# A Nystrom attention and expert block on one core: the routing loss from products over tokens, the inverse in pairs of rounds

## The chip, the cores and the metric

The kernel runs on one core of one Trainium2 chip. A core has TensorE (matmuls, PE), VectorE (DVE), ScalarE (ACT), GpSimd (POOL) and SyncE (SP, which issues DMAs). Matmuls write to PSUM, eight banks of 2 KB per partition; everything else lies in SBUF, 128 partitions. All data are fp32, and an fp32 matmul stands in the trace as two passes, each with its own weight load (PEld). The metric is device microseconds of one execution.

## The reference

The input is x of 16 batches, 1024 tokens, 256 features. Two residual layers follow each other:

```python
x = x + layernorm(attn(layernorm(x)))
x = x + layernorm(ffn(layernorm(x)))
```

The attention is Nystrom's, with 16 heads of 16 features and 64 landmarks (means over 16 neighbouring tokens). Three softmax kernels are formed, k1 (tokens by landmarks), k2 (landmarks by landmarks) and k3 (landmarks by tokens), and k2 is inverted by six rounds:

```python
V = K.T / max(colsum(K))
for _ in range(6):
    KV = K @ V
    V = 0.25 * V @ (13*I - KV @ (15*I - KV @ (7*I - KV)))
out = (k1 @ V) @ (k3 @ v) @ w_proj
```

The second layer chooses one of eight experts per batch, by how well a small autoencoder of each expert reconstructs the normalised tokens, and adds that expert's adapter to a common base layer:

```python
h = relu(x @ Wd1[e] + bd1[e])            # 256 -> 64, for all 8 experts
recon = h @ Wd2[e] + bd2[e]              # 64 -> 256
idx = argmin_e mean((recon - x)**2)      # per batch
out = x @ W_base + b_base + relu(x @ Wa_down[idx] + ba_down[idx]) @ Wa_up[idx] + ba_up[idx]
```

## The kernel before

The work of a batch is written as four stages, each a Python generator. `stage_a` turns the normalised x, makes queries, keys and values, and sums k3 against the values. `stage_p` forms k2 and inverts it. `stage_c` forms k1, multiplies, projects, normalises and adds. `stage_d1` normalises again and computes the eight losses, the choice and the gathers of the expert's weights; `stage_d2` computes base and adapter, normalises, adds and stores.

Each stage yields, ahead of a piece of work, a tuple from `go(...)`: its name, the pieces it follows, and its costs on the engines (`mm(us, mode, n)` for TensorE, `ew(engine, us, ...)` for others). At the end of the kernel a planner (`Model`, `first`, `planned`, lines 1089 to 1210) merges the stages of different batches into one order: it tries each piece that may come next, runs its model forward for `AHEAD` us under a few rules, and takes the piece that loses least TensorE time. The order is then emitted as it stands (`tc.manual_schedule`), so each engine's queue has this order. There are five streams (line 1053): stage a of all batches, stage p of the even batches, stage p of the odd batches, stage c, and stages d1 and d2. PSUM tiles come from one pool of four buffers of two banks (`ps2`), taken in turn.

TensorE's array is used in several tile shapes, which the trace gives as rows*columns: 128*128, 64*64 (four products side by side), 32*128 and 128*32 (four), 128*64 (two).

In `stage_p` a head's matrix is 64 by 64, and 16 heads lie in one [128, 8, 64] tile. `product` (line 552) multiplies all 16 heads, 32 passes of 64 columns in 64*64 tiles; it can place its result in one or the other half of the partitions, which the next product's operands need. A round (line 630) has the steps kv (two products, K V placed in two ways, then two subtractions from 7/3 of the identity on VectorE, yx and yy), sq (one product), t3 (one product) and v (two products, V and its transpose, each scaled by ScalarE). Every step waits for the one ahead of it. Tiles of stage p carry the batch's parity in their tags, so that two batches have their own.

In `stage_d1` the hidden layer is made per pair of experts: `hidden` (line 895) writes ph, 128 hidden units by 1024 tokens, and ScalarE applies bias and relu (ht, line 907). Then for each pair, half of the features and half of the tokens, a group pr (line 932) of eight passes reconstructs two experts' 128 features of 512 tokens, VectorE subtracts xt (df, line 940) and ScalarE squares with a bias and sums along the row (line 943, with a second instruction that reads the accumulator). A batch has four ph groups and 16 pr groups. `pe` (line 961) adds the sums per expert, a matmul with ones (pl, line 966) adds over partitions, and the choice and the gathers on GpSimd follow.

Ahead of the first batch the weights are loaded on ScalarE's DMA queue and the first x on SyncE's; VectorE centres w_proj and w_base (lines 154 to 156), and two small transposes bring the biases into columns (line 192).

## Time and profile before

| | |
|---|---|
| median of three runs | 2420.9 us (2420.38 to 2425.7) |
| profiled execution, its own time | 2422.45 us |
| its span | 2420.7 us |
| PE / PEld busy | 2220.6 us (92%) / 1458.7 us (60%) |
| DVE / ACT / POOL busy | 1475.8 (61%) / 1241.5 (51%) / 272.2 us (11%) |
| mean granted clock of TensorE | 0.978 |
| loss: pr (L932), df (L940), squares (L943) busy | 251.0 PE, 301.7 DVE, 363.3 ACT us |
| hidden layer: ph (L899), ht (L907) | 236.3 PE, 70.8 ACT us |
| inverse: the products of the six rounds (L563, without pkt) | 380.5 us PE, in 18432 passes |

Busy time of a group counts an instruction from its start to its modelled end. Matmuls overlap their successors, so groups of PE add up to more than the time they take from their start to the next group's start; the timeline shows the latter. The granted clock is the share of TensorE's full clock that the chip let through. "Idle before" a group is put down to what ended last.

### The profile page before, as it was taken

To read this page: it belongs to the slowest core of one execution; us is meant where nothing else is said; L and a number is where in the kernel's file an instruction comes from. 1 tells how busy PE (TensorE), PEld (TensorE's weight loads), DVE (VectorE), ACT (ScalarE), POOL (GpSimd) and SP (SyncE) were. 2 spreads that over 40 slices of the span, in tenths; PEclk is the share of its full clock that TensorE was granted. 3 is DMA by queue.
4 is the path that set the end of the run, shared out by engine and by line. 5 is a ranking of instruction groups with operands and counts; after the bars stand their busy time and mean duration, and the time that the engine had idled before them with its cause. 6 is when DMAs were issued, how large, how long until landed. Compare 5 with 4: busy or idle time off the path is not lost.

```text
span 2420.7 us, 94984 instructions
## 1 busy us (share of the span) xinstructions
PE 2220.6 (92%) x43954; PEld 1458.7 (60%) x43954; DVE 1475.8 (61%) x2811; ACT 1241.5 (51%) x2467; POOL 272.2 (11%) x387
## 2 busy tenths in 40 slices
PE   5998999999999999999999999899999999898865
PEld 3666656575565756657565665656666575665442
DVE  4556576575747666576566657557575666655443
ACT  1333464564546556464745545455454555465545
POOL 1000011020110201011020200202011020111021
PEclk9999999999999999999999999999999999999888
DMA  3000001010010100101010010101001000010000
GB/s 109 19 21 3 20 5 55 2 34 25 5 54 3 57 2 5 54 6 54 2 57 2 14 45 3 55 3 32 27 5 55 2 21 21 5 38 26 15 21 20
DMA packets 56628, 60.94 MB, mean 25 GB/s; under 512 B 4964, under 2 KB 55208, under 8 KB 56232
## 3 DMA queue, kind: packets, MB, share of 16 engines
q1 hardware_dynamic: 50208, 50.35, 6.5%
q8 instruction: 345, 5.65, 0.9%
q0 software_dynamic: 2560, 2.14, 0.3%
q10 hardware_dynamic: 3464, 2.37, 0.3%
q14 instruction: 51, 0.42, 0.1%
HBM read 38.08 MB, written 16.78 MB: 23 GB/s over the span
## 4 chain that ended last, share of the span: by engine, by line
PE 43%; DVE 8%; ACT 7%; issue 2%; POOL 1%; DMA 0%; POOLq 0%; DVEq 0%; ACTq 0%
PE ph L899 5%; PE pq L339 5%; PE pr L932 4%; ACT df L943 3%; PE pf L1033 3%; PE po L829 2%; PE pv L360 2%; PE pvi L563 2%; PE pf L1034 2%; PE pkv L563 2%; PE psv L781 2%; PE psct L752 2%; DVE df L940 2%; DVE mx L417 1%; PE psct L760 1%
## 5 line engine op out<-in xcount | busy, mean ns | idle before, releaser
L943 ACT ACTIVATE df<-df,bd_sb 128x512 f32<-128x512 f32 x512 | 363.3, 711 | 165.4 <-DVE df L940 165.4
L940 DVE TENSOR_TENSOR df<-pr,xt_d 128x1024 f32<-128x1024 f32 x256 | 301.7, 1216 | 107.9 <-PE pr L932 68.5
L932 PE MATMUL pr<-ht,wd_sb 64*64 64x512 f32 x2048 | 251.0, 597 | 3.6 <-ACT ht L907 1.5
L899 PE MATMUL ph<-xt_d,wd_sb 128*128 128x512 f32 x512 | 236.3, 604 | 1.4 <-DVE maxima L722 0.8
L339 PE MATMUL pq<-xt_a,wqkv_sb 128*128 128x512 f32 x512 | 228.1, 600 | 0.0
L722 DVE TENSOR_REDUCE maxima<-psc 128x16 f32<-128x1024 f32 x128 | 150.3, 1217 | 76.9 <-PE psc L714 76.9
L770 ACT ACTIVATE e<-psct 128x1024 f32<-128x1024 f32 x128 | 124.0, 1020 | 115.3 <-PE psct L760 115.2
L417 DVE TENSOR_REDUCE mx<-psm 128x2 f32<-128x1024 f32 x128 | 149.7, 1216 | 33.5 <-PE psm L408 33.5
L339 PEld LDWEIGHTS pq<-xt_a,wqkv_sb 128*128 128x128 f32 x512 | 96.0, 192 | 114.3 <-issue 110.0
L899 PEld LDWEIGHTS ph<-xt_d,wd_sb 128*128 128x128 f32 x512 | 93.1, 191 | 117.1 <-issue 94.6
L453 ACT ACTIVATE e<-psc 128x1024 f32<-128x1024 f32 x128 | 122.8, 1025 | 73.2 <-PE psc L443 71.8
L1033 PE MATMUL pf<-wbase_sb,xt_d 128*128 128x256 f32 x512 | 136.6, 390 | 0.9 <-DVE t L659 0.9
L563 PEld LDWEIGHTS pkv<-vi,k2t 64*64 64x64 f32 x6144 | 104.1, 137 | 44.1 <-issue 18.2
L283 DVE SCALAR_TENSOR_TENSOR y_d<-y_d,rstd_d_y,x 128x256 f32<-128x256 f32 x128 | 53.3, 479 | 124.2 <-POOL rstd_d_y L250 124.1
L248 POOL TENSOR_SCALAR ve_c_y<-ss_c 128x4 f32<-128x4 f32 x32 | 6.2, 195 | 1086.6 <-ACT square_c L294 1086.6
L563 PE MATMUL pkv<-vi,k2t 64*64 64x64 f32 x6144 | 115.1, 223 | 8.0 <-ACT vi L673 3.3
L932 PEld LDWEIGHTS pr<-ht,wd_sb 64*64 64x64 f32 x2048 | 64.9, 133 | 95.5 <-issue 60.6
L829 PE MATMUL po<-wproj_sb,svt 128*128 128x256 f32 x512 | 120.1, 388 | 1.0 <-ACT svt L804 0.9
L781 PE MATMUL psv<-w_bd,e 128*32 128x34 f32 x8192 | 90.3, 198 | 33.0 <-issue 23.5
L781 PEld LDWEIGHTS psv<-w_bd,e 128*32 128x32 f32 x8192 | 80.0, 109 | 61.7 <-issue 35.7
L360 PE MATMUL pv<-wqkv_sb,xt_a 128*128 128x256 f32 x512 | 116.7, 381 | 0.0
L360 PEld LDWEIGHTS pv<-wqkv_sb,xt_a 128*128 128x128 f32 x512 | 95.9, 190 | 22.5 <-issue 7.8
(174 smaller groups left out, 4042.8 us busy)
## 6 DMA issues: line engine op xcount, KB each, us to landing
xa<-in_L_attn_x_dram SPq DMA_DIRECT2D x16, 1024.0 KB
x<-in_L_attn_x_dram SPq DMA_DIRECT2D x16, 1024.0 KB
out_dram<-y_d SPq DMA_DIRECT2D x32, 512.0 KB
wqkv_sb<-in_L_attn_w_qkv_dram ACTq DMA_DIRECT2D x1, 768.0 KB
wd_sb<-in_L_ffn_Wd_dram ACTq DMA_DIRECT2D x2, 256.0 KB
wd_sb<-in_L_ffn_Wd_dram ACTq DMA_DIRECT2D x1, 512.0 KB
wdn<-in_L_ffn_Wa_down_dram,row POOLq DMA_INDIRECT x32, 2.7
wproj_sb<-in_L_attn_w_proj_dram ACTq DMA_DIRECT2D x1, 256.0 KB
```

The costliest lines, as they stand in the source:

```text
L339: nc.tensor.matmul(pq[:, n, :], lhsT=wqkv_sb[:, k, f0 : f0 + P], rhs=xt[:, k, n * 512 : (n + 1) * 512], start=(k == 0), stop=(k == NC - 1),)
L360: nc.tensor.matmul(pv[:, j, :], lhsT=xt[:, k, (t0 + j) * P : (t0 + j + 1) * P], rhs=wqkv_sb[:, k, 2 * D : 3 * D], start=(k == 0), stop=(k ...
L417: nc.vector.tensor_reduce(mx3[:, n, q : q + 2], psc[g], X, ALU.max)
L563: nc.tensor.matmul(dst[64 * h[to] : 64 * h[to] + 64, 4 * h[frm] + 2 * g0 + g1, :], lhsT=x[rows, i, :], rhs=y[rows, j, :] if y_at else y[ro ...
L722: nc.vector.tensor_reduce(mx[:, t0 : t0 + 2, 64 * g : 64 * g + 64].rearrange("x t (p j) -> x p t j", p=2)[:, :, :, 0 : 2 * NC], psc[g].rea ...
L781: nc.tensor.matmul(psv[rows32(g), j // 2, col : col + 2 * (HD + 1)], lhsT=es[p // 2][:, p % 2, j * P + 32 * g : j * P + 32 * g + 32], rhs= ...
L829: nc.tensor.matmul(po[:, j, :], lhsT=svt[n][:, c, j * P : (j + 1) * P], rhs=wproj_sb[:, c, :], start=(c == 0), stop=(c == NC - 1),)
L899: nc.tensor.matmul(ph[:, n, :], lhsT=wd1_sb[:, k, 2 * i : 2 * i + 2, :].rearrange("p e h -> p (e h)"), rhs=xt[:, k, n * 512 : (n + 1) * 51 ...
L932: nc.tensor.matmul(pr[to, r, :], lhsT=wd2_sb[half, i, k * P + 64 * f : k * P + 64 * f + 64], rhs=ht[half, cols], start=True, stop=True,)
L940: nc.vector.tensor_tensor(df, pr, middle(xt[:, k, cols], 2), ALU.subtract)
L943: nc.scalar.activation(df[:, r, :], df[:, r, :], AF.Square, bias=bd2_sb[:, e, k : k + 1], accum_out=part[:, e, k * NW + n : k * NW + n + 1],)
L1033: nc.tensor.matmul(po[:, j, :], lhsT=xt[:, k, cols], rhs=wbase_sb[:, k, :], start=(k == 0), stop=False)
```

## The change

The loss is computed from products over tokens. With g = max(h, -bd1), which is relu(h + bd1) - bd1, a constant vector c = bd1 Wd2 + bd2 per expert, and x the normalised tokens, the squared error summed over tokens is made of g'g (64 by 64 per expert) weighted by Wd2 Wd2', g'x (64 by 256) weighted by -2 Wd2, the sums of g and of x weighted by vectors, and the sum of x squared. `hidden` now puts tokens on partitions (128 tokens by 512 hidden units of all experts) and VectorE writes the maximum into one of two tiles g0, g1, which have a column of ones behind each expert's 64. `over_tokens` makes, for a window of 512 tokens and four experts, the pg group: two experts side by side in 128*64 tiles, 256 columns against x and 65 against g with its ones, summed over four token tiles in PSUM. VectorE multiplies the result by the weights `loss_w` in place, and ScalarE sums along the rows. Sums of x come from the copies of xt (now two per window, with a sum), sums of squares from the variances. `prepare_d` makes the weights once.

The inverse treats its rounds in pairs. An even round keeps X = K V and forms t3 as before, but in place of the next K V it multiplies X by t3 (step x); the odd round then needs no product with K. The second placement of y is no longer a product: ScalarE copies two halves across partitions (`across`). Stage p of all batches is one stream, and its tiles are no longer kept per parity.

The rest: the first x comes in two loads; centring and the bias transposes move into the planned order (`prepare_c`, `prepare_d`); wd2 lies in a buffer of tag e1 that is released afterwards; the planner looks 70 us ahead, and for the last 250 us of TensorE's work to the end, with four more rules there.

```diff
-AHEAD, GAP = 50.0, 1.0
+AHEAD, LAST, GAP = 70.0, 250.0, 1.0
...
-        nc.sync.dma_start(out=t, in_=x[b].rearrange("(t p) d -> p t d", p=P))
+        rows = x[b].rearrange("(t p) d -> p t d", p=P)
+        for h in range(2 if b == 0 else 1):
+            part = slice(0, NT) if b else slice(4 * h, 4 * h + 4)
+            nc.sync.dma_start(out=t[:, part, :], in_=rows[:, part, :])
...
-    wd2_sb = const.tile([P, E // 2, D], F32, name="wd2_sb")
+    wd2_sb = work.tile([P, E // 2, D], F32, tag="e1", name="wd2_sb")
...
-    for c in range(NC):
-        centre(wproj_sb[:, c, :])
-        centre(wbase_sb[:, c, :])
...
+    loss_w = const.tile([P, E // 2, LW], F32, name="loss_w")
+    loss_x = const.tile([P, NC, E], F32, name="loss_x")
+    loss_b = const.tile([P, E], F32, name="loss_b")
+    halfmask = groups("halfmask", 2)
+    minus_bd1 = const.tile([P, E, 64], F32, name="minus_bd1")
+    nc.scalar.dma_start(out=minus_bd1.rearrange("p e h -> p (e h)"), in_=bd1.rearrange("(o e) h -> o (e h)", o=1).to_broadcast([P, E * 64]))
+    nc.vector.tensor_scalar(minus_bd1, minus_bd1, -1.0, None, ALU.mult)
+    gs = [const.tile([P, 4, E, 65], F32, name=f"g{i}") for i in range(2)]
+    for t in gs:
+        nc.gpsimd.memset(t.rearrange("p j e h -> p (j e h)"), 1.0)
+    def prepare_c():
+        yield go(("c", 0, "weights"), [("a", 0, "qk", 0, 0)], ew("dve", 1.9, None))
+        for c in range(NC):
+            centre(wproj_sb[:, c, :])
...
+        w2t_ps = two_banks([P, E // 2, NC, P], "w2t_ps")
+        for i in range(E // 2):
+            for k in range(NC):
+                nc.tensor.transpose(w2t_ps[:, i, k, :], wd2_sb[:, i, k * P : (k + 1) * P], ident)
...
+        nc.scalar.mul(loss_w[:, :, 65:LW], wd2_sb, -2.0)
...
+        ww_ps = one_bank([P, E // 2, P], "ww_ps")
+        for i in range(E // 2):
+            for k in range(NC):
+                nc.tensor.matmul(ww_ps[:, i, :], lhsT=w2t[:, i, k, :], rhs=w2t[:, i, k, :], start=(k == 0), stop=(k == NC - 1))
...
+            if squares is not None:
+                mv, rstd = stats[h]
+                nc.vector.tensor_tensor(squares[:, h, :], mv[:, :, 1], rstd, ALU.mult)
+                nc.vector.scalar_tensor_tensor(squares[:, h, :], squares[:, h, :], float(D), rstd, ALU.mult, ALU.mult)
...
+            for k in range(NC):
+                nc.scalar.activation(
+                    xt[:, k, h * 512 : (h + 1) * 512],
+                    pt[:, k].rearrange("p j c -> p (j c)"),
+                    AF.Copy,
+                    accum_out=sums[:, k, h : h + 1],
+                )
...
-        x, y = "r", "s"
...
+        f, h, g = "t", "r", "s"
+        def taken_y(px, scale):
+            y = mat("yx")
+            if scale == 1.0:
+                nc.vector.tensor_tensor(y, px, middle(eyes[0], NP), ALU.subtract)
+            else:
+                nc.vector.scalar_tensor_tensor(y, px, scale, middle(eyes[0], NP), ALU.mult, ALU.subtract)
+            return y
+        def across(y):
+            other = mat("yc", "across")
+            frm, to = (t.rearrange("x (f k p) m -> x f k (p m)", f=2, k=2) for t in (y, other))
+            for r, half in halves():
+                nc.scalar.copy(to[64 - 64 * r : 128 - 64 * r, :, r, :], frm[half, :, 1 - r, :])
+            return y, other
+        ACROSS = ew("act", 0.33, -1, "aside"), ew("act", 0.33, -1, "aside")
         for i in range(N_ITER):
-            yield step(f"kv{i}", mm(2 * Q, "q64", 128), ew("dve", 0.6, 0), ew("dve", 0.6, 0, "free aside"))
...
+            if i % 2 == 0:
+                n = 2 if i == 0 else 1
+                yield step(
+                    f"kv{i}",
+                    mm(n * Q, "q64", 64 * n),
+                    ew("dve", 0.6, 0),
+                    ew("act", 0.5, 0, "aside" if i == 0 else "free aside"),
+                    *([ew("act", 0.5, 0, "free aside")] if i == 0 else []),
+                    *ACROSS,
+                )
+                px, pvt = banks_of(f"pkv{i}")
+                x_at = product(px, (k2t, kt_at), (vi, v_at), h, (g, "p2"))
+                if i == 0:
+                    vt_at = product(pvt, (vi, v_at), (eye, None), h, (g, "p2"))
+                y = taken_y(px, 1.0)
+                xh = mat("xx")
+                nc.scalar.copy(xh, px)
+                if i == 0:
+                    vt = mat("vt")
+                    nc.scalar.copy(vt, pvt)
+                y = across(y)
+            yield step(f"sq{i}", mm(Q, "q64", 64), ew("dve", 0.6, -1, "free"))
             psq = banks_of(f"psq{i}")
-            sq_at = product(psq[0], (yx, at_x), (yx, at_x), y, ("p2", "t"))
+            sq_at = product(psq[0], (y[0], x_at), (y[0], x_at), g, ("p2", f))
             sq = mat("vi", "sq")
             nc.vector.tensor_tensor(sq, psq[0], middle(eyes[1], NP), ALU.subtract)
-            if i == 0:
-                vt = mat("vt")
-                nc.scalar.copy(vt, pvt[1])
             yield step(f"t3{i}", mm(Q, "q64", 64), ew("dve", 0.6, -1, "free"))
             pb = banks_of(f"pb{i}")
-            t3_at = product(pb[0], (sq, sq_at), (yy, at_y), x, ("p2", "t"))
-            t3 = mat("yx", "t3")
+            assert x_at == (h, (f, g, "p2"))
+            t3_at = product(pb[0], (sq, sq_at), ((*y, h), (g, (f, h, "p2"))), h, ("p2", f))
+            t3 = mat("vi", "t3")
             nc.vector.tensor_tensor(t3, middle(eyes[2], NP), pb[0], ALU.subtract)
-            more = i < N_ITER - 1
...
+            if i % 2 == 0:
+                yield step(f"x{i + 1}", mm(2 * Q, "q64", 128), ew("dve", 0.65, 0), ew("act", 0.5, 0, "free aside"), *ACROSS)
+                px, pv = banks_of(f"px{i}")
+                x_at = product(px, (xh, x_at), (t3, t3_at), g, (f, "p2"))
+                vt_at = product(pv, (t3, t3_at), (vt, vt_at), g, (f, "p2"))
+                f, h, g = h, g, f
+                y = taken_y(px, 0.25)
+                vt = mat("vt")
+                nc.scalar.mul(vt, pv, 0.25)
+                y = across(y)
+            else:
+                more = i < N_ITER - 1
+                yield step(
+                    f"v{i + 1}",
+                    mm(*((2 * Q, "q64", 128) if more else (Q, "q64", 64))),
+                    ew("act", 0.5, 0),
+                    ew("act", 0.5, 0, "free aside" if more else "free"),
+                )
+                pv = banks_of(f"pvi{i}")
+                if more:
+                    v_at = product(pv[0], (vt, vt_at), (t3, t3_at), g, (f, "p2"))
+                vt_at = product(pv[1], (t3, t3_at), (vt, vt_at), f, (g, "p2"))
+                if more:
+                    vi = mat("vi")
+                    nc.scalar.mul(vi, pv[0], 0.25)
+                vt = mat("vt")
+                nc.scalar.mul(vt, pv[1], 0.25)
+                f, h, g = g, f, h
...
+        QC = 2
+        def hidden(n, q):
+            yield go(
+                ("d", b, "g", n, q), [("d", b, "xt", n)], mm(3.44, "full", 16), ew("dve", 1.13, -1, "free")
+            )
+            ph = two_banks([P, QC, E * 64], f"ph_{b}_{n}_{q}")
+            for j in range(QC):
+                t = 4 * n + QC * q + j
                 for k in range(NC):
                     nc.tensor.matmul(
-                        ph[:, n, :],
-                        lhsT=wd1_sb[:, k, 2 * i : 2 * i + 2, :].rearrange("p e h -> p (e h)"),
-                        rhs=xt[:, k, n * 512 : (n + 1) * 512],
+                        ph[:, j, :],
+                        lhsT=xt[:, k, t * P : (t + 1) * P],
+                        rhs=wd1_sb[:, k].rearrange("p e h -> p (e h)"),
                         start=(k == 0),
                         stop=(k == NC - 1),
                     )
-            ht = work.tile([P, N], F32, tag="ht", name=f"ht_{b}_{i}")
...
+            nc.vector.tensor_tensor(
+                gs[n % len(gs)][:, QC * q : QC * q + QC, :, 0:64],
+                ph.rearrange("p j (e h) -> p j e h", h=64),
+                minus_bd1.unsqueeze(1).to_broadcast([P, QC, E, 64]),
+                ALU.max,
+            )
+        def over_tokens(n, w):
+            yield go(
+                ("d", b, "fw", n, w),
+                [("d", b, "g", n, q) for q in range(4 // QC)],
+                mm(4.4, "c64", 128),
+                ew("dve", 0.8, -1),
+                ew("act", 0.9, -1, "free"),
+            )
+            g = gs[n % len(gs)]
+            pf = two_banks([P, 2, 512], f"pg_{b}_{n}_{w}")
+            for i in range(2):
+                for cols, own in ((slice(65, LW), False), (slice(0, 65), True)):
+                    for j in range(4):
                         for r, half in halves():
+                            e = 4 * w + 2 * i + r
                             nc.tensor.matmul(
-                                pr[to, r, :],
-                                lhsT=wd2_sb[half, i, k * P + 64 * f : k * P + 64 * f + 64],
-                                rhs=ht[half, cols],
-                                start=True,
-                                stop=True,
+                                pf[half, i, cols],
+                                lhsT=g[:, j, e, 0:64],
+                                rhs=g[:, j, e, :] if own else xns[n][:, j, :],
+                                start=(j == 0),
+                                stop=(j == 3),
                             )
-                    df = buf4k("df", [P, 2, 512], f"df_{b}_{i}_{k}_{n}", 3)
...
+            fw = pf[:, :, 0:LW]
+            nc.vector.tensor_tensor(fw, fw, loss_w[:, 2 * w : 2 * w + 2, :], ALU.mult)
+            for i in range(2):
+                nc.scalar.activation(fw[:, i, :], fw[:, i, :], AF.Copy, accum_out=part[:, n, 2 * w + i : 2 * w + i + 1])
+        yield from hidden(0, 0)
+        yield from hidden(0, 1)
+        yield from hidden(1, 0)
+        yield from over_tokens(0, 0)
+        yield from over_tokens(0, 1)
+        yield from hidden(1, 1)
+        yield from over_tokens(1, 0)
+        yield from over_tokens(1, 1)
+        yield go(("d", b, "fixed"), [("d", b, "xt", h) for h in range(NW)], ew("dve", 0.8, None))
+        fixed = small.tile([P, E], F32, tag="fixed", name=f"fixed_{b}", bufs=1)
+        xsum = small.tile([P, NC + 1], F32, tag="xsums", name=f"xsums_{b}", bufs=1)
+        nc.vector.tensor_reduce(xsum[:, 0:NC], sums, X, ALU.add)
...
-    RANKS = 0, 1, 1, 2, 3
+    RANKS = 0, 1, 2, 3
     def streams():
-        return [
...
+        return [chain(stages) for stages in ([stage_a], [stage_p], [stage_c], [stage_d1, stage_d2])]
...
+            ending = model.done() > TOTAL - LAST
+            limit = TOTAL * 2 if ending else model.clock["pe"] + AHEAD

```

## The prediction

> **What bounds the kernel now.** I read the page's busy table first, then the busy time by stretches, then the groups by line, the waits of TensorE in the middle stretch, and last the timeline, because only the timeline gives the price of a matmul group from its own start to the next start.
>
> ```profile
> span 2420.7 us, 94984 instructions
> PE 2220.6 (92%) x43954; PEld 1458.7 (60%) x43954; DVE 1475.8 (61%) x2811; ACT 1241.5 (51%) x2467; POOL 272.2 (11%) x387
> ```
> ```profile
> 0.00:26.10 26.10, 3.86 (x19) 3.76 (x20) 11.07 (x51) 2.53 (x4) 7.18 (x23) 1.00 0.70 212
> ...
> 60.00:2230.00 2170.00, 2049.39 (x42421) 1360.83 (x42418) 1362.97 (x2578) 1138.38 (x2235) 238.18 (x328) 0.99 0.07 23
> 2230.00:2421.00 191.00, 135.22 (x1356) 76.45 (x1356) 83.80 (x160) 92.85 (x221) 26.84 (x36) 0.85 0.08 24
> ```
> TensorE carries the time: it is busy for 92% of the span. What it loses is 22 us at the head, 121 us (2170 - 2049) over the long middle, and 56 us in the last 191 us, where its granted clock also falls to 0.85. The third row's columns are length, PE, weight loads, DVE, ACT, POOL, clock, DMA share, GB/s.
>
> ```profile
> PE psv L781 <- issue: 23.5, 19, 2.3
> PE pb L563 <- DVE sq L651: 9.0, 8, 1.9
> PE pf L1034 <- POOL a_t L1011: 7.8, 2, 5.7
> PE pvi L563 <- DVE t L659: 5.6, 9, 1.1
> ```
> These are the largest waits of TensorE between 60 and 2230 us (total, times, longest). All that end with "issue" add up to 44 us; the other 77 us are many short waits on VectorE and ScalarE, mostly under 1 us. No single wait is there to be removed.
>
> ```profile
> L943 ACT ACTIVATE df<-df,bd_sb 128x512 f32<-128x512 f32 x512 | 363.3, 711 | 165.4 <-DVE df L940 165.4
> L940 DVE TENSOR_TENSOR df<-pr,xt_d 128x1024 f32<-128x1024 f32 x256 | 301.7, 1216 | 107.9 <-PE pr L932 68.5
> L932 PE MATMUL pr<-ht,wd_sb 64*64 64x512 f32 x2048 | 251.0, 597 | 3.6 <-ACT ht L907 1.5
> ```
> The loss of stage d is the largest customer of all three engines, and it is what the change replaces. The prices come from these rows (start, duration, group):
>
> ```profile
> 1035.87 1.11 PE L563 MATMUL pkv<-vi,k2t 64*64 64x64 f32 x64
> 1036.80 1.90 PE L932 MATMUL pr<-ht,wd_sb 64*64 64x512 f32 x16
> 1038.52 0.64 PE L563 MATMUL psq<-yx 64*64 64x64 f32 x32
> 1038.99 1.04 PE L932 MATMUL pr<-ht,wd_sb 64*64 64x512 f32 x8
> ...
> 1085.58 1.94 PE L1015 MATMUL pad<-xt_d,wdn 128*64 128x512 f32 x8
> 1087.45 0.33 PE L498 MATMUL pm<-ident,maxima 128*128 128x128 f32 x1
> 1087.71 1.16 PE L563 MATMUL pkv<-vi,k2t 64*64 64x64 f32 x64
> 1088.80 1.14 PE L432 MATMUL psc<-mrow,ones 32*128 32x512 f32 x8
> ...
> 1097.24 1.03 PE L1033 MATMUL pf<-wbase_sb,xt_d 128*128 128x256 f32 x4
> 1098.10 0.60 PE L1034 MATMUL pf<-wup,a_t 67*128 67x256 f32 x2
> ```
> Start to start, two pr groups (x16) take 1.72 us, so 0.86 each; one 64x64 product takes 0.47 (psq), two take 0.93 (pkv). The same pkv takes 1.09 when its neighbours use another tile shape: a change of tile shape costs 0.16 us. Four passes of 256 columns take 0.86, so 0.215 each. The pad group, whose tiles are 128*64 as the new loss uses them, takes 1.87 with shape changes on both sides, so 1.71 for four pairs of 512 columns, 0.43 a pair: the two column halves run together and the loads of their weights hide.
>
> **The change, part by part.** All per execution, 16 batches.
>
> Inverse (stage p): products per batch go from 36 to 27. Before, each of six rounds has 2 + 1 + 1 + 2; after, even rounds have 1 + 1 + 1 + 2 and odd ones 1 + 1 + 2; in both, the last round has one less and the first one transpose more. 144 products at 0.464 us leave: -67 us. The steps of the serial chain go from 24 to 21 per batch.
>
> Loss: 256 pr groups at 0.86 leave: -220 us. In their place come 64 pg groups of 16 pairs of 256 columns and 16 pairs of 65 columns. A 256 pair is taken at 0.215; a 65 pair at 0.058 (0.464/8, the product's eight rounds of 64 columns with 64-column weights). 3.44 + 0.93 = 4.37 us, times 64: +280 us. Its lower bound is the pad row's speed over 321 columns, 16 x 321 x 0.43/512 = 4.31. Its upper bound leaves every weight load in the open: loads of 128 columns take 190 ns and of 64 columns 137 in the groups, so 64 columns are worth 53 ns, 32 of them 1.7 us: 6.07 us. I take 4.37, since pad is the same tile shape. The hidden layer's 64 ph groups stay eight passes of 512 columns each.
>
> The Trainium skill, "TensorE: Matmul & The Clock Gate", Part 3, says that a weight load overlaps running matmuls only when it targets other rows of the array; both halves of pg use all 128 rows. By that rule, and the same page's one column per 1/1.2 ns for a load, a group would be dearer by an estimated 32 x 53 ns = 1.7 us and the sum by 109 us. The pad row speaks against it at 512 columns; no row shows it at 65.
>
> Tile-shape changes: pr has the same 64*64 tiles as the products, pg has not. Counted in the order of TensorE's instructions, the changes go from 857 to 997: 140 x 0.16 = +22 us (at least 15, by the 0.11 us between a product left in the same shape and one that is not). The one-time preparation (8 transposes, 32 small matmuls; the 8-transpose group of ptsv takes 1.0 us) adds about 5 us. TensorE's own work thus grows: -67 - 220 + 280 + 22 + 5 = **+20 us**.
>
> Instruction supply: 345 instruction packets served 94,984 instructions; TensorE issues 320 fewer per batch (576 less for products, 256 more for pg), some 20 packets. At 44/345 = 0.13 us of "issue" wait each, -3 us (0 to -15).
>
> ScalarE loses 363 us of squares, their 96 us of accumulator reads, 71 us of ht and 28 us of scalings; it gains 128 sums of 321 columns (about 0.5 + 0.19 us, between the 256- and 512-column rows: 88), split copies of xt_d with a read each (+17), 192 half copies at about 0.38 (72) and 48 copies xh at 0.59 (28): -353 us. VectorE loses 302 us of df and 65 us of yy; it gains 64 maxima of 1024 columns at 1.22 (78), 64 products of 642 columns at 0.85 (54) and small sums (about 34): -201 us. These lie beside TensorE's work; what they are worth is what they take out of the 77 us of short waits. Both engines keep in-order queues, and with VectorE going from 61% to about 53% and ScalarE from 51% to about 38% busy, I take half: -38 us. Ends: -77 (all gone) and +30, because the inverse now runs as one chain where two batches alternated, and a pg group holds its banks for 4.4 us plus about 2.1 us of VectorE and ScalarE, against 0.86 plus 1.2 for pr. In the order, one to three other groups stand between two steps of the chain; a step takes 1.6 us in the tail's timeline (2230.77, 2232.36, 2233.95), so the cover is mostly longer than the step.
>
> Tail: the last batch's inverse (until pw at 2235.35) ran with 0.9 us waits at each step; in the new order three ph groups, two pg groups and the transposes of batch 14 stand among its steps, and behind it the final projection of batch 14 no longer competes with the last normalisation, which TensorE awaited for 11.2 us. I take -12 us, from +5 to -30. The last batch's own loss stays about as long: it was held by ScalarE's squares and is now held by TensorE.
>
> Head: the first statistics can begin on half a load, but VectorE now has the negation of the broadcast bias ahead of the first normalisation, the last transfer on ScalarE's queue; its neighbour in that queue landed at 19.9 us, and the first transposes began at 22.6. Two more fills of 2080 columns on GpSimd (2.0 us each by the 2296-column one) end before rstd is wanted. SyncE keeps its order of loads and stores. I take 0 (-6 to +3).
>
> Sum: +20 - 3 - 38 - 12 = -33 us against the profiled execution's own 2422.45 us (span 2420.7 and 1.75 around it): 2389.5. That execution lies 1.55 us above the median of the three, so 2388.
>
> **Rivals.** *The pg group is dearer.* Loads show through, or the 65-column part runs badly. It ends slower from 4.37 + 33/64 = 4.89 us per group on; at 6.07 us the time is 2388 + 109 = 2497. For it: no row has 65 columns in this shape. Against: pad, and the products' 58 ns a round. *The relief buys nothing.* Waits stay at 77 us, since they belong to the chain and to bank turnover, or grow by 30 with a single chain: 2426 to 2456. For it: the largest waits are on sq and t, steps of the inverse that remain. Against: these waits are VectorE's queue, which loses 201 us. *The relief buys all of it.* With -77 and -30 in place of -38 and -12 the time is 2331. For it: the planner looks further ahead (70 us, and to the end over the last 250). That the change leaves work on other engines out, without effect on TensorE's path, is the second rival.
>
> **How the numbers follow.** Forecast with its own range 2355 to 2415: 0.51. All relief, 2331: 0.17. No relief or a slower chain: 0.14. Dear pg: 0.12. Within 0.2% (about what a measurement here can tell from no change, 5 us): 0.06. So faster 0.68, same 0.06, slower 0.26. The range 2330 to 2455 leaves out most of the dear pg case and the far end of full relief.
>
> **What would show it.** pg at 4.4 us start to start in the timeline; products at 0.47 to 0.63; PE's summed work up while its idle in the middle stretch is down from 121 to about 80 us; ACT near 890 and DVE near 1275 us busy; first transposes at 17 to 26 us. The prediction is wrong if pg passes 4.9 us, or if the inverse's steps show waits above 1 us on VectorE in every batch.

## The result and the profile after

The changed kernel takes 2408.6 us (median of 13 runs, 2402.3 to 2417.7) against 2424.0 us for the kernel before in the same series (median of 13, 2418.9 to 2432.8). The ratio is 0.9933, 95% interval 0.9918 to 0.9947: 16 us faster, where 33 us were forecast. The profiled executions differ by 9.9 us in span, so that is what the two traces can account for.

The head of the page after, and its busy time by the stretches that were shown of before (columns: length, PE, weight loads, DVE, ACT, POOL, each with its instructions, then clock, DMA share, GB/s):

```profile
span 2410.8 us, 89297 instructions
PE 2236.6 (93%) x41450; PEld 1540.4 (64%) x41450; DVE 1283.5 (53%) x2772; ACT 962.7 (40%) x1929; POOL 279.5 (12%) x389
```
```profile
0.00:26.10 26.10, 4.60 (x19) 4.03 (x20) 9.27 (x41) 3.18 (x3) 10.53 (x25) 1.00 0.72 221
...
60.00:2230.00 2170.00, 2061.58 (x39400) 1424.31 (x39400) 1187.45 (x2540) 898.93 (x1781) 241.75 (x328) 0.99 0.08 23
2230.00:2411.00 181.00, 140.09 (x1868) 94.86 (x1868) 66.47 (x162) 51.73 (x136) 27.24 (x36) 0.89 0.06 19
```

VectorE lost 192 us of work and ScalarE 279 us, yet TensorE's idle time in the long middle went only from 121 to 108 us. From here on the middle is taken from 60 us to 190 us before the end of each span, so that kernels of different length can be compared: 121.3 us idle before, 106.3 after. The four parts of the 9.9 us are then: TensorE's busy time +16.0, idle of the first 60 us +1.1, of the middle -15.0, of the last 190 us -12.0.

The largest waits of TensorE in the middle, after (total, times, longest):

```profile
PE psv L920 <- issue: 15.2, 13, 1.8
PE psq L664 <- issue: 7.1, 6, 1.7
PE px L664 <- DVE t L785: 5.5, 8, 1.6
PE b_ps L250 <- DVE bd_of L246: 4.4, 1, 4.4
PE pl L1123 <- DVE pe L1118: 3.7, 4, 1.5
```

Summed over all rows of this view, the waits that end with "issue" fell from 44.3 to 35.7 us. Those for VectorE, ScalarE and GpSimd, called engine waits below, stood at 71.5 us before and stand at 70.1: VectorE 44.8 and 44.7, ScalarE 18.9 and 25.0, GpSimd 7.8 and 0.4. By the forecast's own reckoning (idle less "issue", which takes in gaps too short for the view) they are 77.0 and 70.6. These were the waits that the relief was to halve. On balance nothing went of the waits for the two engines that were relieved.

The new groups and their price, from the page's groups and the timeline (start, duration):

```profile
L1079 PE MATMUL pg<-xn_d,g 128*64 128x256 f32 x2048 | 245.9, 382 | 1.3 <-ACT e L909 1.0
L1056 DVE TENSOR_TENSOR g<-ph,minus_bd 128x1024 f32<-128x1024 f32 x64 | 78.4, 1225 | 174.8 <-PE ph L1049 174.8
L1087 DVE TENSOR_TENSOR pg<-pg,loss_w 128x642 f32<-128x642 f32 x64 | 53.4, 834 | 199.8 <-PE pg L1079 174.3
L1089 ACT ACTIVATE pg<-pg 128x321 f32<-128x321 f32 x128 | 54.1, 422 | 336.0 <-DVE pg L1087 334.0
```
```profile
1044.81 1.95 PE L1079 MATMUL pg<-xn_d,g 128*64 128x256 f32 x16
1046.59 0.64 PE L1079 MATMUL pg<-g 128*64 128x65 f32 x16
1047.06 1.90 PE L1079 MATMUL pg<-xn_d,g 128*64 128x256 f32 x16
1048.78 0.64 PE L1079 MATMUL pg<-g 128*64 128x65 f32 x16
1049.35 0.69 PE L664 MATMUL psq<-yx 64*64 64x64 f32 x32
```

Between the first two pg starts of 256 columns lie 2.25 us, and between the second of them and the product behind it 2.29 us: 4.54 us with one change of tile shape (0.16), so 4.38 for the group; 4.37 was forecast. The 65-column part takes 0.47 us for eight pairs, 58 ns a pair, so the weight loads of its tiles hide too. pg itself waits for almost nothing (1.3 us in all).

### The profile page after: what moved, and what is told of

Its sections match the earlier page's. It is cut to its first block, busy times and chain, and to the rows that moved or that the text cites. A ratio compares the mean times of both kernels' runs of the same rounds, so it can differ in the third digit from the quotient of the medians.

```text
span 2410.8 us, 89297 instructions
## 1 busy us (share of the span) xinstructions
PE 2236.6 (93%) x41450; PEld 1540.4 (64%) x41450; DVE 1283.5 (53%) x2772; ACT 962.7 (40%) x1929; POOL 279.5 (12%) x389
## 4 chain that ended last, share of the span: by engine, by line
PE 78%; DVE 12%; ACT 6%; issue 3%; DMA 1%; POOL 1%; SPq 0%; POOLq 0%; DVEq 0%; ACTq 0%
PE pg L1079 12%; PE ph L1049 9%; PE pq L438 8%; PE pf L1190 5%; PE po L968 5%; PE pv L459 4%; PE psv L920 2%; PE psc L531 2%; PE psct L891 2%; PE pf L1191 2%; DVE mx L516 2%; PE put L570 2%; PE psc L542 2%; PE psm L507 2%; PE psc L853 2%
## 5 line engine op out<-in xcount | busy, mean ns | idle before, releaser
L1079 PE MATMUL pg<-xn_d,g 128*64 128x256 f32 x2048 | 245.9, 382 | 1.3 <-ACT e L909 1.0
L1049 PE MATMUL ph<-wd_sb,xt_d 128*128 128x512 f32 x512 | 232.7, 602 | 0.1
L1089 ACT ACTIVATE pg<-pg 128x321 f32<-128x321 f32 x128 | 54.1, 422 | 336.0 <-DVE pg L1087 334.0
L1079 PEld LDWEIGHTS pg<-xn_d,g 128*64 128x64 f32 x2048 | 136.7, 137 | 70.9 <-issue 6.3
L1056 DVE TENSOR_TENSOR g<-ph,minus_bd 128x1024 f32<-128x1024 f32 x64 | 78.4, 1225 | 174.8 <-PE ph L1049 174.8
L1087 DVE TENSOR_TENSOR pg<-pg,loss_w 128x642 f32<-128x642 f32 x64 | 53.4, 834 | 199.8 <-PE pg L1079 174.3
L1049 PEld LDWEIGHTS ph<-wd_sb,xt_d 128*128 128x128 f32 x512 | 94.5, 192 | 102.0 <-issue 98.9
L968 PE MATMUL po<-wproj_sb,svt 128*128 128x256 f32 x512 | 121.3, 391 | 5.0 <-ACT svt L943 3.8
L968 PEld LDWEIGHTS po<-wproj_sb,svt 128*128 128x128 f32 x512 | 96.7, 194 | 21.9 <-ACT svt L943 5.3
L1142 POOL DMA_INDIRECT wdn<-in_L_ffn_Wa_down_dram,row x32 | 32.8, 1026 | 658.0 <-DVE svn L931 138.4
L1190 PEld LDWEIGHTS pf<-wbase_sb,xt_d 128*128 128x128 f32 x512 | 94.8, 189 | 20.7 <-issue 5.8
```

Of the source, the lines that this page charges most:

```text
L968: nc.tensor.matmul(po[:, j, :], lhsT=svt[n][:, c, j * P : (j + 1) * P], rhs=wproj_sb[:, c, :], start=(c == 0), stop=(c == NC - 1),)
L1049: nc.tensor.matmul(ph[:, j, :], lhsT=xt[:, k, t * P : (t + 1) * P], rhs=wd1_sb[:, k].rearrange("p e h -> p (e h)"), start=(k == 0), stop=( ...
L1056: nc.vector.tensor_tensor(gs[n % len(gs)][:, QC * q : QC * q + QC, :, 0:64], ph.rearrange("p j (e h) -> p j e h", h=64), minus_bd1.unsquee ...
L1079: nc.tensor.matmul(pf[half, i, cols], lhsT=g[:, j, e, 0:64], rhs=g[:, j, e, :] if own else xns[n][:, j, :], start=(j == 0), stop=(j == 3),)
L1190: nc.tensor.matmul(po[:, j, :], lhsT=xt[:, k, cols], rhs=wbase_sb[:, k, :], start=(k == 0), stop=False)
```

## The experiments

The runs of this section were made on four chips. On two of them the kernel before takes 2425 and 2428 us, near the 2424 of the result above, at a granted clock near 0.98; on the other two it takes 2502 to 2504 us at 0.96. The table marks the first kind A and the second B; each ratio is taken to the kernel before on the same chip. The columns after the ratio come from one profiled execution each, in us; the middle runs from 60 us to 190 us before the end, and "engine waits" are the sums described above, over this middle.

How well one profile repeats is seen where two runs have the same order of TensorE's work in the middle. e6 and e14, both on chips B, are 1.8 us apart in idle and 0.9 in engine waits; e11 and e18, both on A, 1.6 and 2.3. Between the kinds of chip the engine waits of one kernel stay (before 71.5 and 72.6, changed 70.1 and 68.4), but the idle time does not (before 121.3 and 153.7).

| kernel | chip | ratio to before (95%) | TensorE busy | middle idle | last 190 us idle | engine waits |
|---|---|---|---|---|---|---|
| before | A | 1 | 2220.6 | 121.3 | 54.8 | 71.5 |
| changed | A | 0.9933 (0.9918-0.9947) | 2236.6 | 106.3 | 42.8 | 70.1 |
| e9 load put back | A | 1.0172 (1.0153-1.0192) | 2246.7 | 144.2 | 45.4 | 106.0 |
| e10 before, new planner | A | 1.0024 (1.0011-1.0037) | 2235.3 | 129.5 | 50.8 | 69.1 |
| e11 changed, old planner | A | 1.0083 (1.0065-1.0101) | 2243.6 | 130.6 | 49.9 | 84.3 |
| e12 two chains, three halves | A | 0.9997 (0.9985-1.0009) | 2223.4 | 135.6 | 42.0 | 77.9 |
| e17 inverse alone, relieved | A | 0.9832 (0.9811-0.9853) | 2167.3 | 132.9 | 51.6 | 90.3 |
| e18 as e11, again | A | 1.0088 (1.0075-1.0102) | 2236.3 | 132.2 | 47.7 | 86.6 |
| e5 before again | B | 0.9985 (one run) | 2266.2 | 153.7 | 53.8 | 72.6 |
| e1 ScalarE relieved | B | 0.9954 (0.9937-0.9971) | 2269.4 | 150.0 | 51.1 | 64.8 |
| e2 both relieved | B | 0.9883 (0.9857-0.9908) | 2257.4 | 139.5 | 48.2 | 60.5 |
| e3 one chain | B | 1.0148 (1.0119-1.0177) | 2291.0 | 176.6 | 52.1 | 85.8 |
| e4 inverse alone | B | 0.9965 (0.9948-0.9983) | 2228.9 | 181.8 | 54.8 | 112.5 |
| e6 changed again | B | 0.9893 (0.9872-0.9914) | 2270.1 | 134.8 | 42.6 | 68.4 |
| e7 changed, one g tile | B | 0.9983 (0.9967-0.9999) | 2277.6 | 148.4 | 44.8 | 78.3 |
| e8 two chains, one g tile | B | 0.9918 (0.9892-0.9943) | 2255.2 | 153.1 | 43.7 | 72.9 |
| e13 50 us ahead | B | 0.9916 (0.9886-0.9946) | 2268.1 | 151.8 | 43.3 | 85.5 |
| e14 70 us ahead, no end rule | B | 0.9926 (0.9900-0.9951) | 2272.7 | 133.0 | 48.3 | 67.5 |
| e15 60 us ahead | B | 0.9978 (0.9965-0.9991) | 2276.4 | 156.5 | 41.9 | 81.1 |
| e16 100 us ahead | B | 0.9890 (0.9869-0.9912) | 2262.1 | 141.1 | 43.1 | 81.0 |

**What is the relief worth by itself?** e1 and e2 keep every instruction of TensorE and their order, and shorten the loss's passes on the other engines (the rest of the loss is left out).

```diff
-nc.vector.tensor_tensor(df, pr, middle(xt[:, k, cols], 2), ALU.subtract)
+few = slice(n * 512, n * 512 + 64)
+nc.vector.tensor_tensor(df[:, :, 0:64], pr[:, :, 0:64], middle(xt[:, k, few], 2), ALU.subtract)   # e2 only
 nc.scalar.activation(
-    df[:, r, :], df[:, r, :], AF.Square, ...
+    df[:, r, 0:64], df[:, r, 0:64], AF.Square, ...
```

> The kernel before, with ScalarE's squares over 64 of the 512 columns (448 of 512 left out of the loss; order, waits and all other work as before). By the 711 ns of a square and 0.83 ns a column from the 256- and 512-column rows, ScalarE loses some 190 us of its 1242. The relief theory (half of TensorE's short waits hang on how busy the other engines are): 10 to 20 us less idle in the middle stretch and some 6 us less at the end, where the last loss is held by the squares; 2400 to 2410 us. The order theory (waits are set by the order and its chains, and by the supply of instructions): the middle stretch's idle stays within 5 us of 121; only the end gains; 2412 to 2420 us.

> As the run before it, and VectorE's subtraction ahead of the squares also over 64 of 512 columns of each half: VectorE loses some 240 us of 1476, ScalarE some 190, about what the change takes from both (192 and 279), with TensorE's work and order unchanged. Relief theory: 30 to 45 us less, 2380 to 2395 us, the middle stretch's idle near 80 us. Order theory: the middle stretch's idle stays above 108 us, 2405 to 2418 us, with what there is at the end.

By their ratios e1 is 12 us faster and e2 29 us (of 2503). The middle rows of before (e5) and of e2, same columns as above:

```profile
60.00:2307.50 2247.50, 2093.82 (x42468) 1387.63 (x42465) 1364.66 (x2580) 1141.02 (x2242) 238.84 (x330) 0.97 0.07 22
```
```profile
60.00:2278.50 2218.50, 2079.02 (x42345) 1384.03 (x42346) 1170.28 (x2575) 981.26 (x2224) 237.10 (x326) 0.97 0.07 22
```

VectorE lost 194 us in the middle and ScalarE 160, and TensorE's idle time there fell by 14 us (2247.50 - 2093.82 = 153.7, 2218.50 - 2079.02 = 139.5). Of these, 12 are engine waits. The rest of the 29 us is the last 190 us (-6) and TensorE's own busy time (-9), whose cause was not traced. By the time e2 lies next to the relief theory (30 to 45 us less), by the middle's idle next to the order theory (at most 13); e1's 4 us of idle are within the order theory's 5. ScalarE's relief is smaller here than in the changed kernel, where it loses 245 us in the middle. So the relief is real, and is worth under half of the forecast's 38 us where the forecast put it. Waits at the inverse's own steps are still there in e2:

```profile
PE pb L563 <- DVE sq L651: 9.2, 7, 2.1
PE psq L563 <- DVE yx L639: 6.4, 5, 3.9
```

Summed over the rows of the view, the products of the rounds (pkv, pvt, psq, pb, pvi, and px of the new inverse) have 33.6 of the 72.6 us of engine waits in e5 and 30.4 of the 60.5 in e2. So the relief took 3 us off there, and 9 off the 39.0 at all other work.

**What does the single chain cost, and the new inverse in it?** e3 is the kernel before with one stream for stage p in place of two (the planner's measure of how far a stream has come changes with it). e4 adds the new inverse to that.

```diff
-RANKS = 0, 1, 1, 2, 3
+RANKS = 0, 1, 2, 3
-return [chain([stage_a]), chain([stage_p], range(0, NB, 2)), chain([stage_p], range(1, NB, 2)),
-        chain([stage_c]), chain([stage_d1, stage_d2])]
+return [chain(stages) for stages in ([stage_a], [stage_p], [stage_c], [stage_d1, stage_d2])]
```

> The kernel before, with the inverse of all batches as one stream in place of one for even and one for odd batches; the loss, the products and the planner's settings as before. Changes of tile shape go from 857 to 929: at 0.16 us +12 us. If one chain costs waits too (a price that the prediction put at up to 30 us): 2435 to 2465. If the chain is covered: 2425 to 2436.

> The kernel before with the new inverse alone, as one stream (the loss, the planner's settings and the preparation as before). 930 changes of tile shape. Against the one-stream run: 144 products at 0.464 us less, -67 us, and the chain three steps shorter; VectorE 65 us less, ScalarE some 80 more. If products count in full: 67 us under the one-stream run, near 2365, and the new loss then costs what lies between this and the 2408 of the changed kernel, some 40 us, as its +60 of TensorE work less its relief would have it. If the new chain is held by the copies across halves, which ScalarE makes: above 2395, and the loss costs little.

e3 is 37 us slower, inside the range for a chain that costs waits. Middle idle rises by 23 us and engine waits by 13; TensorE's busy time rises by 25, of which the 72 more changes of tile shape make 12 at 0.16 each, and the lower clock (0.955 against 0.963) can make the rest. e4 is 46 us faster than e3, not the 67 that 144 fewer products save: its busy time is 62 lower, but engine waits grow by another 27 us. The largest waits in the middle of e4, then one of e3 and the two largest for VectorE in the kernel before (e5), all on the same chip:

```profile
PE psv L819 <- issue: 20.5, 20, 2.1
PE po L867 <- ACT svt L842: 10.4, 6, 6.2
PE put L471 <- issue: 9.4, 13, 2.2
PE psq L565 <- DVE yx L641: 8.1, 9, 1.7
PE pvi L565 <- DVE t L686: 8.0, 7, 4.3
```
```profile
PE psq L563 <- DVE yx L639: 11.8, 13, 4.1
```
```profile
PE pb L563 <- DVE sq L651: 9.7, 8, 1.9
PE psq L563 <- DVE yx L639: 6.5, 8, 2.0
```

The two rises stand in different places. From e5 to e3 the waits at the products of the rounds go from 33.6 to 48.4 us, and those elsewhere do not rise (39.0 and 37.4). From e3 to e4 those at the products fall to 43.7, and those at all other work go up to 68.8; by engine, waits for ScalarE go from 21.8 to 52.7 us and for VectorE from 62.0 to 58.2. The new inverse gives ScalarE more work in the middle (1140.55 us in e3, 1218.36 in e4). Waits of that other work for ScalarE alone rise from 10.5 to 40.3 us, po above among them: the 27 us stand there, and not at the inverse's products. Waits for the copies across halves themselves add up to only 0.5 us, so the rival that expected above 2395 has the time (0.9965 of 2424 is 2416), but not by the wait that it named.

**Does the relief pay for the chain?** e17 is e4 with the loss passes shortened as in e2; TensorE's order is that of e4.

> The kernel with the new inverse as a single chain and the old loss, with the subtraction and the squares run over 64 of the 512 columns; the output is not the reference's, since the rest of the loss is left out. TensorE's instructions and order are those of the run with the inverse alone. Theory that relief and chain act on the same waits: the waits for VectorE, ScalarE and GpSimd fall from 112 to 70 to 85 us, and the time by 35 to 55 us against the run with the inverse alone, ratio to the kernel before 0.975 to 0.983. Rival (the relief is worth here what it is in the kernel before): the waits fall by under 15 us and the time by 20 to 32 us, ratio 0.984 to 0.989.

The time falls by 1.33% against e4, 32 us (on chips of different kind), and engine waits from 112.5 to 90.3. By the time it is the upper end of the rival (20 to 32 us; the ratio, 0.9832, lies between the two ranges), by the waits it is neither: 22 us went, more than the 12 in the kernel before, but not the 27 to 42 of the theory that relief and chain act on the same waits. The middle row of e17:

```profile
60.00:2186.90 2126.90, 1994.04 (x37581) 1286.69 (x37575) 1114.53 (x2475) 1056.22 (x2417) 237.81 (x328) 0.99 0.08 23
```

e9 tries it from the other side: the changed kernel with work put back on both engines behind each loss step. To make room it also has three half g tiles that rotate in place of two whole ones; no wait of TensorE in its middle is put down to g, but this part was not run by itself.

```diff
+for _ in range(4):
+    nc.scalar.copy(junk[0], minus_bd1.rearrange("p e h -> p (e h)"))
+for _ in range(3):
+    nc.vector.tensor_scalar(junk[1], minus_bd1.rearrange("p e h -> p (e h)"), -1.0, None, ALU.mult)
```

> The changed kernel with work put back on the two engines that it relieved: behind each of its 128 loss steps ScalarE copies 512 columns four times and VectorE scales 512 columns three times, into scratch that nobody reads; TensorE's instructions and their order stay (997 changes of tile shape). ScalarE should then be busy some 1200 us and VectorE some 1450, as in the kernel before. Prediction's theory (the relief is worth 38 us in the middle and 12 at the end): 35 to 50 us slower than the changed kernel, ratio to the kernel before 1.003 to 1.009. Theory from the two relief runs on the kernel before (the relief is worth 29 us, most of it not in the waits the prediction counted): 20 to 32 us slower, ratio 0.997 to 1.002. Rival (in the new kernel nothing waits for the passes): within 8 us, ratio 0.989 to 0.993.

It is 58 us slower than the changed kernel (1.0172 against 0.9933), above every theory's range; middle idle is up 38 us and engine waits 36. The load was put back in lumps:

```profile
L211 ACT COPY junk<-minus_bd 128x512 f32<-128x512 f32 x512 | 316.5, 618 | 13.3
L213 DVE TENSOR_SCALAR junk<-minus_bd 128x512 f32<-128x512 f32 x384 | 162.8, 424 | 8.8
```

Four copies are 2.5 us of ScalarE at a stretch, where two squares were 1.4, so this run says that such work is not hidden in the new kernel; that it overstates what the relief is worth fits the lumps, but was not tested. Taken with the order kept, the relief is worth 12 us of engine waits in the kernel before (e2) and 22 with the new inverse in one stream (e17 against e4).

**Is the single chain a loss in the new kernel too?** Two streams with the new loss need more SBUF than two g tiles leave, and the new loss beside the old inverse was not run, so the loss alone has no price here. e7 has one g tile, so that the second 512 tokens begin after the first's last expert group; e8 is e7 with two streams. e5 and e6 are the yardsticks.

> The kernel before, unchanged, for a profile on the chip of the experiments. Both theories: ratio 1.00; TensorE busy within 10 us of 2220 between head and tail, and idle in the middle 100 to 140 us, the yardstick for the single-chain kernels.

> The changed kernel, unchanged, timed beside the experiments. Both theories: ratio 0.993 to 0.995 to the kernel before (12 to 18 us faster).

> The changed kernel with one g tile in place of two: the second window of 512 tokens enters its first product only after the last expert group of the first. This alone is the base for the next run. TensorE's own work is unchanged (997 changes of tile shape, as in the changed kernel). Both theories: 0 to 8 us slower than the changed kernel, since a group of the loss can wait for the tile while the three other streams go on.

> The same as the run with one g tile, but the inverse again as two streams of batches that alternate, each with its own buffers (the freed tile makes room for them). Single-chain theory: 20 to 37 us faster than the run with one g tile (872 changes of tile shape against 997, at 0.16 us 20 us; the rest from shorter waits for VectorE and ScalarE in the middle), so some 2375 to 2395 against the 2409 of the changed kernel, ratio to the kernel before 0.980 to 0.988. Rival (the chain is covered by the other streams once the products are cheaper, and the relief itself is not worth anything beside the new loss): within 6 us of the run with one g tile, and idle time in the middle unchanged within 5 us.

e5 and e6, on a chip B, fell outside what both theories expected (TensorE's busy time, the idle, and 0.9893 for the ratio). e8 is 18 us faster than e7 (2478.5 against 2496.9), just short of the single-chain theory's 20 to 37 and outside the rival's 6. Its busy time is 22 us lower, for 125 fewer changes of tile shape (20 us at 0.16), but its middle idle is 5 us higher: engine waits are 5 lower, waits put down to "issue" 10 higher (68.1 and 78.6).

```profile
60.00:2305.00 2245.00, 2096.60 (x39298) 1451.58 (x39299) 1184.90 (x2531) 897.74 (x1774) 237.99 (x328) 0.97 0.07 22
```
```profile
60.00:2285.10 2225.10, 2071.97 (x39230) 1447.72 (x39231) 1185.73 (x2522) 894.01 (x1766) 235.76 (x324) 0.97 0.07 22
```

And e7 itself is 22 us slower than the changed kernel (e6), where 0 to 8 were expected. e12 makes room for two streams without that loss: three half g tiles that rotate, the mirrored copy of y packed into half its size, small buffers shared, and 843 changes of tile shape against 997.

```diff
-gs = [const.tile([P, 4, E, 65], F32, name=f"g{i}") for i in range(2)]
+gs = [const.tile([P, 2, E, 65], F32, name=f"g{i}") for i in range(3)]
...
-other = mat("yc", "across")
+other = inv.tile([P, NP // 2, M], F32, tag=f"yc{b % 2}", name=f"across_{b}")
```

> The changed kernel with the inverse again as two alternating streams, and room made for their buffers: the two g tiles become three halves that rotate, the mirrored copy of y is kept packed, and small buffers are shared. 843 changes of tile shape against 997. Theory that a single chain costs own work of TensorE: 154 x 0.16 us = 25 us less, 18 to 32 us faster than the changed kernel, ratio to the kernel before 0.976 to 0.982, idle time about unchanged. Rival (another order gives back in waits what it saves in changes): within 8 us of the changed kernel, ratio 0.986 to 0.993.

It was to be 18 to 32 us faster than the changed kernel and is 16 us slower, equal to the kernel before. TensorE's own work did fall, by 13 us; the middle idle rose by 29, of which 8 are engine waits and 19 "issue" (35.7 and 55.0):

```profile
60.00:2234.20 2174.20, 2038.58 (x39341) 1427.18 (x39342) 1181.21 (x2523) 892.93 (x1763) 235.12 (x324) 0.98 0.08 23
```

So the two pairs disagree on the time. In the clean one, e7 and e8, two streams win 18 us, all of it in TensorE's busy time; in the other, e12, which also changes the g tiles, the same saving is lost again in waits. That the single stream costs the new kernel more waits in all, as it did in e3, is shown by neither.

**How much is the planner, and the order it happens to give?** e10 is the kernel before with the new planner, e11 and e18 the changed kernel with the old one, and e13 to e16 the changed kernel with other constants.

```diff
-AHEAD, LAST, GAP = 70.0, 250.0, 1.0
+AHEAD, LAST, GAP = 50.0, -1.0, 1.0    # e11, e18: no end rule
+AHEAD, LAST, GAP = 50.0, 250.0, 1.0   # e13
+AHEAD, LAST, GAP = 70.0, -1.0, 1.0    # e14: no end rule
+AHEAD, LAST, GAP = 60.0, 250.0, 1.0   # e15
+AHEAD, LAST, GAP = 100.0, 250.0, 1.0  # e16
```

> The kernel before with the planner of the changed kernel alone: 70 us ahead in place of 50, and the last 250 us looked through to the end with rules that spread the streams; 864 changes of tile shape against 857. Theory that the tail's gain is the planner's: 8 to 14 us faster than the kernel before, ratio 0.9945 to 0.997, the idle time of the last 190 us down by that. Rival (the tail's gain comes from the shorter loss passes): within 5 us, ratio 0.998 to 1.002.

> The changed kernel with the planner of the kernel before: 50 us ahead, no special end; 974 changes of tile shape against 997. Theory that the tail's gain is the planner's: 5 to 14 us slower than the changed kernel, ratio to the kernel before 0.991 to 0.995. Rival: within 5 us of it, ratio 0.987 to 0.991; the 23 fewer changes would give 4 us.

> The changed kernel with 50 us of looking ahead and the special end kept; 980 changes of tile shape. Order theory (each setting is a draw): anywhere from 0 to 40 us slower than the changed kernel, mostly by idle time in the middle. End theory (the special end was the planner's worth): within 10 us of the changed kernel, ratio to the kernel before 0.990 to 0.997. Look-ahead theory (70 is needed): as slow as with the old planner, ratio 1.004 to 1.010.

> The changed kernel with 70 us of looking ahead and no special end: the order of the middle is that of the changed kernel. All theories of the middle: middle idle within 5 us of the changed kernel's 106 us. End theory: 10 to 35 us slower. Look-ahead and order theories: 3 to 12 us slower, from the tail alone, ratio to the kernel before 0.994 to 0.999.

> The changed kernel with 60 us of looking ahead; 981 changes of tile shape. Order theory: ratio to the kernel before between 0.99 and 1.01 with no trend in the look-ahead. Look-ahead theory: between the settings 50 and 70, ratio 0.996 to 1.004.

> The changed kernel with 100 us of looking ahead; 971 changes of tile shape. Order theory: ratio to the kernel before between 0.99 and 1.01, as likely slower than the changed kernel as with 60. Look-ahead theory: as fast as the changed kernel or faster, ratio 0.985 to 0.994.

> The changed kernel with the old planner, once more. If the chip makes the difference, a chip where the kernel before takes 2500 us gives a ratio of 0.992 to 0.997, and one where it takes 2425 us gives 1.006 to 1.010. If the order and the end make it, 1.006 to 1.010 on either.

The planner's settings are no gain for the kernel before: e10 is 6 us slower, where the tail theory expected 8 to 14 faster and its rival no change. Its last 190 us lose 4 us of idle, its middle gains 8. On the changed kernel and chips A they decide its sign: with the old planner it is 20 us slower than before (e11; e18 on another chip of the same kind gives 21), 36 us from the changed kernel, where no theory expected more than 14. The middle row of e18:

```profile
60.00:2248.60 2188.60, 2056.40 (x39415) 1430.56 (x39415) 1190.23 (x2540) 898.35 (x1782) 237.37 (x328) 0.98 0.08 23
```

TensorE's busy time in the whole span is that of the changed kernel (2236.3 and 2236.6), and its middle idle is 26 us higher. Without the end rule the last 190 us lose 6 us (48.3 of idle in e14 against 42.6 in e6) and the ratio goes from 0.9893 to 0.9926, with intervals that overlap. Over the look-ahead, at 50, 60, 70 and 100 us, the ratio on chips B goes 0.992, 0.998, 0.989, 0.989 and the middle idle 151.8, 156.5, 134.8, 141.1. From 50 to 60 it gets slower, from 60 to 70 faster, and 70 and 100 agree within their intervals, so this is no trend: the look-ahead theory falls with e13 (0.9916, where it expected 1.004 or more) and the end theory with e14 (8 us slower than the changed kernel, where it expected 10 to 35); the order theory is left, whose ranges were wide. A constant that changes no computation moves the time by up to 22 us on chips B. None of these kernels is faster than the changed one by more than the interval.

e11 and e13 differ only in the end rule, worth 6 to 8 us, but stand at 1.008 on chips A and 0.992 on a chip B. Their middles have the same order, and the same engine waits (84.3 and 86.6 in e11 and e18, 85.5 in e13). The chip makes some 0.4% for the changed kernel (0.9933 and 0.9893) and the end rule some 0.3%, which leaves 0.9% of the 1.7% unexplained; this pair was not run on one kind of chip.

## Why the prediction was right in sign and wrong in size

*TensorE's own work, +20 us.* Measured +16.0 in the two profiles of the result, and +3.9 on a chip B (e5 and e6); one profile each does not tell how much of this is the clock. The pg group (4.37 forecast, 4.38 measured) and its 65-column part (58 ns a pair) were read rightly from the pad and the product rows, and the rival of a dearer pg is out. The Trainium skill, "TensorE: Matmul & The Clock Gate", Part 3, has a list of what overlaps, by which a weight load overlaps running matmuls only when it targets other rows. The timeline above shows pairs of 58 ns on the same 128 rows, so here the measurement decides against that rule.

*Instruction supply, -3.* The "issue" waits fell by 9 us in the middle, inside the range, and the instruction packets from 345 to 325, as counted. That the one comes of the other is not shown, and the fixed price per packet does not hold: e10, with the 345 packets of before in another order, has 57.0 us of these waits against 44.3.

*Head, 0.* First transposes at 21.5 us against 22.6 before; idle of the first 60 us +1.1.

*Tail, -12.* Measured -12.0 in the last 190 us, so the sum is right; it has more sources than the two that were named, and their shares are not settled: e2 took 6 there by relief alone, and e14 lost 6 there without the end rule.

*Other engines.* VectorE came out as forecast (1283 against some 1275 us). ScalarE was to be near 890 and is 963. The forecast took 353 us off its busy time by adding rows, but ScalarE's rows overlap: the trace of before has squares at 1039.77, 1040.49, 1041.19, 1041.89 us, 0.70 apart with the read of the accumulator inside, where the rows add to 0.71 + 0.19. Its rows add to 1381 us against 1241.5 busy. The rows' difference is indeed 351 us (1381 to 1030), the busy time's 279.

*The middle, -38: the step that failed.* The prediction took half of 77 us of short waits away because VectorE and ScalarE were relieved, and put the single chain at nothing, as an end of +30 only. The middle as a whole gave 15 us; 9 of them are "issue", so the term of -38 measured -6 (77.0 to 70.6). On a chip B the same two kernels give -7 (77.8 to 70.7, e5 and e6).
- The reason given against the second rival, that "these waits are VectorE's queue, which loses 201 us", does not hold. VectorE's waits are what they were (44.8 and 44.7 us), ScalarE's have grown (18.9 to 25.0), and 8 of the 77 us were GpSimd's, the pf row of the prediction; those went. With VectorE's relief, two thirds of ScalarE's and the order kept (e2) only 12 of 73 us of engine waits went, and only 3 of the 34 at the products of the rounds. That those stand for the way from a product through one operation and back, which a shorter queue does not shorten, fits this but was not measured by itself.
- What was put at nothing was not nothing. One stream on the old kernel puts 13 us on the engine waits (e3), and the cheaper products in it another 27 (e4), and these stand not at the chain's products but at other work that waits for ScalarE (10.5 to 40.3 us). Relief then takes 22 off again (e17), the rest of the new loss with the old planner 4 to 6 (e11, e18), and the new planner's order 14 to 17. By these steps 73 becomes 86, 113, 90, 84 to 87, and 70. Only the steps of the relief and the repeats keep the order; the planner's constants alone moved the engine waits by up to 18 us on chips B (67.5 to 85.5), so the 13 alone could be another order, the 40 of both together are more than that.
- In the changed kernel the products of the rounds wait 22.9 us where they waited 31.0, a fall no larger than that of their number (27 for 36), and all other work waits 47.2 where it waited 40.5. With the old planner these are 37.9 and 46.4 (e11).
- The order was given no term, and it is as large as the disputed one. The middle idle of the changed kernel is 106 us with its own planner and 131 with the old one on chips A; four look-aheads span 22 us on chips B. So what is missing of the 38 us cannot be split for certain between the chain's price, ScalarE's added work and the order drawn.

The rival "the relief buys nothing" describes the engine waits of the changed kernel best, but for another reason than it named: in e2 and e17 the relief bought something, and e3 and e4 show new waits that can take it back. Its 2426 to 2456 us were missed as well, because TensorE's own work came out 4 us lower than in the sum, the "issue" waits gave 6 us more, and the term itself 6.

*The clock* had no term either. By the two profiles 53 us of full clock were not granted before (0.022 of 2420.7) and 43 after (0.018 of 2410.8): 10 us less, as much as the spans differ, with 8 of them in the last 190 us (0.85 and 0.89 granted). Over the fast runs it was 0.983 for the changed kernel and 0.977 for the kernel before on chips A, 0.972 to 0.974 with the old planner. Whether a higher clock made a part of the gain, or came of fewer waits, no run here separates.

## What to carry to other kernels

Waits of a serial chain for a half-idle engine need not be its queue: lightening both engines removed 3 of 34 us at the chain's own products here, and 9 of 39 elsewhere. When a change both relieves engines and gives up a second stream, price the two separately, each on the kernel before, ahead of adding them, and split the waits by engine and by place before they are given one name. Where a planner makes the order, an edit draws a new order, and its spread (here 22 to 36 us, found by varying constants that compute nothing) belongs in the range of a forecast.

## What the runs showed of the hardware that was not expected

The same kernel takes 2425 us on some chips and 2503 us on others, 3.2% apart, with granted clocks of 0.978 and 0.96; the waits put down to "issue" in the middle are 44 us on the one and 76 us on the other. Ratios move with it: the change gives 0.9933 on the one kind and 0.9893 on the other, with intervals that do not meet. So a gain below one per cent that was measured on one chip was not the same on the other kind.

A change of TensorE's tile shape cost 0.18 us each in the pair e7 and e8 (22.4 us of busy time for 125 of them), close to the 0.16 read from single places, but 0.09 between the changed kernel and e12 (13.2 us for 154), whose profile has a slightly lower clock (0.979 against 0.982).
